# Head 0 of a graph attention layer aggregated in the last head's order

## The chip, the core and the metric

The kernel runs on one core of a Trainium2 chip. The time is the device time in microseconds of one execution; the number of a kernel is the median over several. TensorE is called PE in the profile (PEld its weight loads), VectorE DVE, ScalarE ACT, GpSimd POOL and SyncE SP. SP issues most DMAs.

## The reference, cut to what matters

There are 512 nodes of 768 features and 8704 edges. Two graph attention layers follow each other, the first with 8 heads of 768 features, the second with one; a residual and a layer norm close it.

```
h = (x @ W).reshape(n, H, C)
alpha_s = jnp.einsum('nhc,hc->nh', h, a_s)
alpha_d = jnp.einsum('nhc,hc->nh', h, a_d)
e = jax.nn.leaky_relu(alpha_s[src] + alpha_d[dst], NEG_SLOPE)
...                                     # softmax of e over the edges of each dst
msg = h[src] * alpha[:, :, None]
out = jax.ops.segment_sum(msg, dst, num_segments=n)
...
h = jax.nn.elu(gat_layer(x, W1, a_src1, a_dst1, b1, ...))
out = gat_layer(h, W2, a_src2, a_dst2, b2, ...)
x = layernorm(x + out)
```

## The kernel before

The edges are counted into a dense 512 x 512 matrix `cnt` (rows are dst, four tiles of 128), so a head's softmax is a dense one over rows and its aggregation a matrix product. Four steps belong to a head: the projection x W1, the logits (a product with a_s and a_d, summed along the features, on DVE), the softmax, and the aggregation, followed by elu and by the product with the head's 768 rows of W2, which is added into `h2`. All products are cut into 2 x 2 blocks (for heads 1 to 6 some into 3 x 3) and done with fewer block products than there are pairs of blocks. With 2 x 2 there are seven, P1 to P7; P1 and P2 take blocks of the operands as they are, and most of the others take sums and differences. Each block product sits in a PSUM bank of the pool `mm` (five banks); P2 is added into P1's bank, P4 into P7's and P3 into P5's.

The order of the work is written out by hand: each engine runs its instructions in the order in which the code issues them, and semaphores hold back an instruction whose inputs are not ready.

The softmax of one tile t goes through `lift` (the scores, ACT, L636), `leak` and `rank` (DVE, L640 and L645, with an exponential on ACT at L651), `weigh` (DVE, L879 to L883), a scaling on ACT (L899), a copy that splits the numbers in halves (L902), a transposing DMA on SP (L904) and `turn_in` (ACT, L907), which writes the tile's columns of `PT`. `rank` adds `absent`, which is large where there is no edge. It is made on ACT from `cnt`; for t = 2 at L566, from a difference that DVE takes at L565.

The aggregation of head 0 and of heads 1 to 6 is `mixed` (L949). It runs over c = 0, 1, 2, a chunk of 128 features in each half. `left_sums` (L932 to L935) makes sums of the head's features, `right_sums` (L943 to L946) sums of `PT`: t1, t2, the difference that is written over `PT`, and t4. P1 and P2 need only the columns `near` of `PT`, those of tiles 0 and 1; the sums need all four tiles. Per c the order on PE is P1, P6, P7, P2, P5, P4, P3. ACT copies P1 to `u` (L974); DVE adds P6 (L980) and P7 (into `w`, L981), subtracts `w` from P5 into the far half of `zr` (L986), adds `u` to P4 (L989) and subtracts `u` from P3 (L993). `elu` (L910) is two relus and an exponential on ACT (L916 to L918) and one DVE instruction into `gT` (L919). For the near half of the first chunk it is called at once; those of `zr` and of the far half of `u` are called in the next c:

```
            nc.scalar.copy(u, part("P1"))
            if h == c == 0:
                logarithm(slice(1, NT))
            if behind:
                behind = behind[0]()
            tt(u, u, part("P6"), op=ALU.add)
```

`logarithm` (L657) turns `cnt` into its logarithm, which the softmax of the later heads uses. ACT loads another table for it, and the old one again for the next exponential. In head 0 one tile of it stands in front of the stage and three behind the first copy to `u`.

Head 7 has a function of its own, `last_mixed` (L1001). It issues the sums of the right side first, then P1 of c = 0 and 1, then P2 of c = 0 and 1 with their elu, and then P6, P7, P5, P4 and P3 of c = 0 and 1, and c = 2 as a whole.

DVE work that isn't part of a head's aggregation is dealt into gaps: `half_logits` gives the two logits of one tile of the next head (L418). The logits of head 1's tile 2 are `some_logits`; those of tiles 0, 1 and 3 are `sources` (a_s) and `targets` (a_d). `row_out` (L622) sends the a_s logits through DRAM into a broadcast tile `q`: a small transpose on DVE (L625), four DMAs (L628) and one back (L631). On SP the loads of head 2's first weights (L109, L114) and vectors follow them.

After the aggregation of head 0 comes its product with W2 (`by_halves`, L409 in the profile), with sums on DVE (L389 to L392 for `gT`, L401 and L402 for the weights), and then the projection of head 2.

Of the kernel before, what the change touches and what calls it, by code (L numbers as in the profile page):

```python
# [13 lines left out]
AF = mybir.ActivationFunctionType  # L14
# [6 lines left out]
NO_EDGE = -1e30  # L21
# [16 lines left out]
def gat_pass(  # L38
# [16 lines left out]
    nc = tc.nc  # L55
    P = 128
    N, D = x.shape
    H = a_src1.shape[0]
    E = src.shape[0]
    NT = N // P  # L60
# [232 lines left out]
    far = const.tile([P, 1], F32, name="far")  # L293
# [75 lines left out]
    cnt = keep.tile([P, NT, N], F32, name="cnt")  # L369
    absent = keep.tile([P, NT, N], BF16, name="absent")  # L370
# [183 lines left out]
    def counted(t, ps):  # L554

        nc.scalar.copy(cnt[:, t, :], ps[:, :N])
        nc.scalar.activation(absent[:, t, :], ps[:, :N], AF.Relu, bias=far, scale=NO_EDGE)

    def counted_by_steps(t, ps):


        steps = ohp.tile([P, N + 1], F32, name="steps")
        nc.scalar.activation(steps[:, 1:], ps[:, :N], AF.Copy, scale=0.5)
        nc.scalar.activation(steps[:, :1], ps[:, N - 1:N], AF.Copy, scale=-0.5)
        nc.vector.tensor_tensor(cnt[:, t, :], steps[:, 1:], steps[:, :N], op=ALU.subtract)  # L565
        nc.scalar.activation(absent[:, t, :], cnt[:, t, :], AF.Relu, bias=far, scale=NO_EDGE)  # L566

    def first_projection(h, XA, B_, between):

# [63 lines left out]
    def lift(h, t):  # L633

        q = BC[h] if 0 < h < H and t + 1 == NT else qpool.tile([P, N], F32, name="q")
        nc.scalar.activation(q, BC[h][:, :N], AF.Identity, bias=AL[h][1][:, t:t + 1], scale=-1.0)  # L636
        return q
# [18 lines left out]
    def logarithm(tiles):  # L656
        nc.scalar.activation(cnt[:, tiles, :], cnt[:, tiles, :], AF.Ln, bias=tiny)  # L657
        folded.append(True)
# [19 lines left out]
    if not general:  # L678
# [12 lines left out]
        cps, done = {}, set()  # L691
# [82 lines left out]
        for n, batch in enumerate(batches):  # L774
            for k in sorted({c // quarter for c in batch} - made):
                destinations(k)
                made.add(k)
            if n + 1 < len(batches):
                sources(kinds(batch, False), waiting)
            if n + 2 == len(batches):  # L780
                sources(kinds(batches[-1], False), [])
            ahead = kinds(batches[n + 1], True) if n + 1 < len(batches) else []
            items_here = max(wants[n] - pos if n < len(wants) else 0, 1)
            share = len(ahead) // (items_here + 1) if n == 0 else -(-len(ahead) // items_here)
            waiting = []
            for f in extra.pop(n, []):
                f()
            while n < len(wants) and pos < wants[n]:
                if pos == wholes:
                    pairs = projection(1, XA, B1)  # L790
                    items += [(m, e, False) for m, e in pairs[:4]]
                multiply, empty, on_vector = items[pos]
                multiply()
                if on_vector:
                    waiting.append(empty)
                else:
                    empty()
                pos += 1
                for t, r in turns.get(pos, []):
                    turn_x(t, r)  # L800
                if pos == 1:
                    nc.scalar.activation(nidx, idx, AF.Copy, bias=0.5, scale=-1.0)
                part = 0 if n == 0 and pos == 2 else share
                for c in ahead[:part]:
                    one_hot(c, True)
                del ahead[:part]
            for c in ahead:
                one_hot(c, True)
            if n == 2:
                turn_b1()  # L810
            if n + 1 == len(batches):
                spread(0)
                q = [lift(0, t) for t in range(NT)]
                for t in range(NT - 1):
                    leak(q[t])
                for t in range(NT - 1):
                    rank(q[t], t)
            if n == 0:
                pst = mm.tile([P, 512], F32, name="mm")
                nc.tensor.matmul(pst[:1, :1], found, ones, start=True, stop=True)  # L820
            if n == 3:
                again = nc.values_load(flag[:1, :1], min_val=0, max_val=E)
            count(batch, n + 1 == len(batches))
        assert not extra and not waiting and pos == len(items) and len(done) == NT
    else:
# [26 lines left out]
        q = [lift(0, t) for t in range(NT)]  # L852
# [53 lines left out]
    def turn_in(t):  # L906
        nc.scalar.copy(PT.rearrange("p s n -> p (s n)").bitcast(U16).rearrange("p (s n h) -> p s n h", s=NT, h=2)[  # L907
            :, :, t * P:(t + 1) * P, :], parted.pop(t).rearrange("p (h s d) -> p s d h", h=2, s=NT))
# [40 lines left out]
    def mixed(h, A_, B_, fill, ends=()):  # L949

        tt = nc.vector.tensor_tensor
        behind = []

        def some(c, j):
            for f in fill[c][j]:
                f()

        for c in range(HK):
            u = work.tile([P, HN], F32, name="u")
            w = work.tile([P, HN], F32, name="w")  # L960
            zr = work.tile([P, N], F32, name="zr", bufs=3)
            bank = {}

            def part(p, over=None):
                if over is None:
                    bank[p] = mm.tile([P, 512], F32, name="mm")
                else:
                    bank[p] = bank[over]
                for k in range(2):
                    nc.tensor.matmul(bank[p][:, :HN], A_[p][:, k, c * P:(c + 1) * P], B_[p][:, k, :],  # L970
                                     start=over is None and k == 0, stop=k == 1, skip_group_check=True)
                return bank[p][:, :HN]

            nc.scalar.copy(u, part("P1"))  # L974
            if h == c == 0:
                logarithm(slice(1, NT))
            if behind:

                behind = behind[0]()
            tt(u, u, part("P6"), op=ALU.add)  # L980
            tt(w, u, part("P7"), op=ALU.add)  # L981
            for f in behind[:1]:
                f()
            near_l = elu(h, c, part("P2", over="P1"), near, "l")
            some(c, 0)
            tt(zr[:, far_], part("P5"), w, op=ALU.subtract)  # L986
            for f in behind[1:] + list(ends[:1]) * (c == HK - 1):
                f()
            tt(zr[:, near], u, part("P4", over="P7"), op=ALU.add)  # L989
            near_l()  # L990
            for f in list(ends[1:]) * (c == HK - 1):
                f()
            tt(u, part("P3", over="P5"), u, op=ALU.subtract)  # L993
            some(c, 1)

            def others(c=c, u=u, zr=zr):
                return [elu(h, HK + c, zr, slice(0, N), "r", spare=zr), elu(h, c, u, far_, "l", spare=u)]
            behind = [others]
        return behind[0]()

    def last_mixed(A_, B_, sums, fill):  # L1001

        h, tt = H - 1, nc.vector.tensor_tensor
        banks, us, nears = {}, {}, {}

        def part(c, p, over=None):
# [13 lines left out]
        def near_half(c):  # L1020
            nears[c] = elu(h, c, part(c, "P2", "P1"), near, "l")
# [8 lines left out]
            begin(c)  # L1030
        for c in range(2):
            near_half(c)
        behind = []
        for c in range(HK):
            if c == 2:
# [59 lines left out]
    AA, lsums = left_sums(0)  # L1095
    BB, rsums = right_sums()
    some_logits = half_logits(1, 2)

    def give(t):
        turn_out(q[t], t, weigh(q[t], t, scale=False))  # L1100

    done = {n: (lambda n=n: pairs[n][1]()) for n in range(4, 13)}
    beside = {4: [lambda: give(0)], 5: [done[4]], 6: [done[5]], 7: [done[6], lambda: give(1)],
              8: [done[7], lambda: leak(q[3]), lambda: rank(q[3], 3), lambda: turn_in(0)], 9: [lambda: give(2), done[8]],
              10: [lambda: give(3), lambda: turn_in(1), done[9]], 11: [done[10], lsums[0]],
              12: [done[11], lambda: turn_in(2), *lsums[1:3]], 13: [done[12], lambda: turn_in(3), lambda: logarithm(slice(0, 1)), *rsums[:2]]}
    for n in range(4, 14):
        pairs[n][0]()
        for f in beside[n]:
# [2 lines left out]
            load_w2(0, "w1")()  # L1112
            B2, pending = right(W2[0], "w1")
    pairs[13][1]()
    for f in rsums[2:]:
        f()
    besides = [lsums[3], *some_logits]

    def g_thirds(h):

# [53 lines left out]
    for h in range(H - 1):  # L1174
        last = h + 2 == H
        q = {}
        if 0 < h and not last:
            B3, rest_of_thirds, sums = load_thirds(h + 2)
# [8 lines left out]
        sources, targets = zip(*halves)  # L1187
        row = [lambda: row_out(h + 1)]
        if h == 0:
            GA, gsums = left(gT, gS)  # L1190
            finish = mixed(0, AA, BB, [[[besides[0], sources[1]], [besides[1], sources[0]]], [[], [sources[2]] + row + besides[2:]],
                                       [[], list(targets)]])
            load_w1(2)()
            load_a(2, a_src1[2], a_dst1[2])
            attend = attended(0)
# [8 lines left out]
            gsums[1]()  # L1204
            pending[0]()
            pairs[2][0]()
            gsums[2]()
            pairs[3][0]()
            gsums[3]()
            pending[1]()  # L1210
# [186 lines left out]

    first, second_, third_, fourth = (given(t) for t in range(NT))
    BB, rsums = right_sums()
    finish = last_mixed(AA, BB, [*rsums, lsums[3], lambda: nc.vector.memset(rows, 0.0)], {(1, 1): second_[:1], (2, 1): first})  # L1400
    every = slice(0, N)
    pairs = second(GA, B2)

# [28 lines left out]
    q, rden = {}, {}  # L1432
# [102 lines left out]
```

## Time and profile before

| what | us |
|---|---|
| median of 3 runs | 628.48 (627.97 to 628.87) |
| the profiled execution's own time | 628.25 |
| its span, first to last instruction | 626.5 |
| PE busy in the span | 615.7 |
| DVE busy | 528.8 |
| ACT busy | 339.2 |
| granted TensorE clock | 0.997 |

A row of the timeline reads: start, duration, engine, line, operation, output <- inputs, shapes, how many; a bracket gives the idle time of the engine in front and what ended it. A matmul of the code is two matmul instructions in the profile. A row of the waits reads: who waited for whom, microseconds in total, how often, the longest.

### The profile page before, as it was taken

To read this page: it belongs to the slowest core of one execution; us is meant where nothing else is said; L and a number is where in the kernel's file an instruction comes from. 1 tells how busy PE (TensorE), PEld (TensorE's weight loads), DVE (VectorE), ACT (ScalarE), POOL (GpSimd) and SP (SyncE) were. 2 spreads that over 40 slices of the span, in tenths; PEclk is the share of its full clock that TensorE was granted. 3 is DMA by queue.
4 is the path that set the end of the run, shared out by engine and by line. 5 is a ranking of instruction groups with operands and counts; after the bars stand their busy time and mean duration, and the time that the engine had idled before them with its cause. 6 is when DMAs were issued, how large, how long until landed. Compare 5 with 4: busy or idle time off the path is not lost.

```text
span 626.5 us, 8547 instructions
## 1 busy us (share of the span) xinstructions
PE 615.7 (98%) x2765; PEld 483.6 (77%) x2765; DVE 528.8 (84%) x1125; ACT 339.2 (54%) x602; POOL 148.9 (24%) x177
## 2 busy tenths in 40 slices
PE   8999999999999999999999999999999999999995
PEld 5555576556888888888888888888888888886553
DVE  8988979888899879978799778977898778978785
ACT  5874876650658236651658246751658146754361
POOL 1300011013333234323342323323342313010000
PEclk9999999999999999999999999999999999999998
DMA  8994297789999999999999998999999995590042
GB/s 298 326 235 110 67 265 238 188 216 267 249 222 142 326 256 198 172 274 219 248 237 175 308 250 194 194 283 226 228 215 192 317 280 91 107 261 17 17 76 79
DMA packets 109568, 129.45 MB, mean 207 GB/s; under 512 B 41622, under 2 KB 90446, under 8 KB 108750
## 3 DMA queue, kind: packets, MB, share of 16 engines
q1 hardware_dynamic: 75518, 91.35, 47.3%
q0 software_dynamic: 33568, 36.90, 38.4%
q10 hardware_dynamic: 432, 0.59, 0.3%
q8 instruction: 24, 0.39, 0.3%
q14 instruction: 26, 0.21, 0.1%
HBM read 99.84 MB, written 2.90 MB: 164 GB/s over the span
## 4 chain that ended last, share of the span: by engine, by line
PE 86%; ACT 1%; DMA 1%; DVE 1%; issue 0%
PE mm L480 46%; PE mm L970 20%; PE mm L409 13%; PE mm L1481 3%; PE mm L1012 3%; DMA zr<-pS 0%; DMA zr<-nr 0%; ACT PT L907 0%; ACT pS L902 0%; ACT q L899 0%; PE tr L1390 0%; ACT nr L902 0%; PE tr L891 0%; PE bc L1425 0%; DVE hs L1485 0%; PE tr L1427 0%
## 5 line engine op out<-in xcount | busy, mean ns | idle before, releaser
L486 ACT ACTIVATE hs<-mm 128x512 f32<-128x512 f32 x30 | 17.9, 596 | 86.1 <-PE mm L480 85.8
L970 PE MATMUL mm<-PT,hs 128*128 128x256 f32 x252 | 61.3, 379 | 0.0
L970 PEld LDWEIGHTS mm<-PT,hs 128*128 128x128 f32 x252 | 47.8, 190 | 7.3 <-ACT u L974 0.4
L649 ACT ACTIVATE q<-q,nmax 128x512 f32<-128x512 f32 x32 | 23.1, 721 | 51.2 <-DVE nmax L645 50.8
L493 DVE TENSOR_TENSOR hs<-hs,mm 128x512 f32<-128x512 f32 x45 | 30.9, 686 | 22.1 <-PE mm L480 21.3
L491 POOL DMA_DIRECT2D h<-pass x22 | 26.5, 1319 | 80.9 <-ACT pass L490 80.9
L970 PE MATMUL mm<-pS,gS 128*128 128x256 f32 x168 | 43.2, 380 | 1.3 <-DVE pS L944 1.3
L493 DVE TENSOR_TENSOR h<-h,mm 128x512 f32<-128x512 f32 x56 | 38.3, 684 | 6.3 <-PE mm L480 5.8
L907 ACT COPY PT<-zr 128x1024 uint16<-128x1024 uint16 x34 | 39.3, 1155 | 4.2 <-DMA zr<-pS 3.6
L480 PE MATMUL mm<-w2r,xT 128*128 128x256 f32 x160 | 37.8, 379 | 0.0
L480 PE MATMUL mm<-w2r,gT 128*128 128x256 f32 x160 | 37.0, 379 | 0.0
L970 PEld LDWEIGHTS mm<-pS,gS 128*128 128x128 f32 x168 | 31.8, 190 | 5.9 <-DVE pS L944 1.7
L133 POOL DMA_DIRECT2D w1t<-in_L_gnn_W_dram x18 | 29.2, 1642 | 30.4 <-PE mm L409 26.9
L480 PE MATMUL mm<-w1t,hs 128*128 128x256 f32 x144 | 34.1, 380 | 0.0
L480 PE MATMUL mm<-w1r,hs 128*128 128x256 f32 x144 | 34.1, 379 | 0.0
L480 PE MATMUL mm<-w1r,gS 128*128 128x256 f32 x144 | 34.0, 379 | 0.0
L480 PEld LDWEIGHTS mm<-w2r,gT 128*128 128x128 f32 x160 | 30.4, 190 | 4.1
L480 PEld LDWEIGHTS mm<-w2r,xT 128*128 128x128 f32 x160 | 30.4, 190 | 4.1
L974 ACT COPY u<-mm 128x256 f32<-128x256 f32 x21 | 7.8, 371 | 45.5 <-PE mm L970 45.5
L716 DVE TENSOR_SCALAR os<-nodes,idx 128x512 bf16<-128x512 f16 x104 | 29.3, 354 | 1.4 <-PE tr L742 1.4
L480 PEld LDWEIGHTS mm<-w1t,hs 128*128 128x128 f32 x144 | 27.3, 190 | 3.9 <-ACT absent L490 0.2
L480 PEld LDWEIGHTS mm<-w1r,hs 128*128 128x128 f32 x144 | 27.2, 190 | 3.8 <-DVE hs L1130 0.2
(294 smaller groups left out, 1560.8 us busy)
## 6 DMA issues: line engine op xcount, KB each, us to landing
w2r<-in_L_gnn_W_dram SPq DMA_DIRECT2D x48, 384.0 KB
w1r<-in_L_gnn_W_dram SPq DMA_DIRECT2D x43, 384.0 KB
gT<-xd SPq DMA_DIRECT2D x5, 1280.0 KB
w1t<-in_L_gnn_W_dram SPq DMA_DIRECT2D x24, 256.0 KB
h<-pass POOLq DMA_DIRECT2D x22, 256.0 KB, 4.6
w1t<-in_L_gnn_W_dram POOLq DMA_DIRECT2D x18, 256.0 KB, 6.2
w2t<-in_L_gnn_W_dram SPq DMA_DIRECT2D x15, 256.0 KB
w2t<-in_L_gnn_W_dram POOLq DMA_DIRECT2D x15, 256.0 KB, 9.1
```

Source lines behind the costliest of these rows:

```text
L133: nc.gpsimd.dma_start(o, i, accum_op=ALU.add)
L409: nc.tensor.matmul(ps[:, :HALF], A_[p][:, k, i * P:(i + 1) * P], B_[p][:, k, :], start=start and k == 0, stop=k == HK - 1, skip_group_chec ...
L480: nc.tensor.matmul(bank[chain][:, i * TH:(i + 1) * TH], A_[p][:, k, i * P:(i + 1) * P], B_[p][:, k, :], start=first and i == k == 0, stop= ...
L486: nc.scalar.activation(out(o), ps, AF.Copy, scale=sign)
L491: nc.gpsimd.dma_start(out(o), part, accum_op=ALU.add)
L493: nc.vector.tensor_tensor(out(o), out(o), ps, op=ALU.add if sign > 0 else ALU.subtract)
L649: nc.scalar.activation(q, q, AF.Exp, bias=nmax, scale=-1.0, accum_out=dens[t])
L716: nc.vector.tensor_scalar(o, nodes, idx[:, c:c + 1], None, op0=ALU.is_equal)
L907: nc.scalar.copy(PT.rearrange("p s n -> p (s n)").bitcast(U16).rearrange("p (s n h) -> p s n h", s=NT, h=2)[:, :, t * P:(t + 1) * P, :], p ...
L970: nc.tensor.matmul(bank[p][:, :HN], A_[p][:, k, c * P:(c + 1) * P], B_[p][:, k, :], start=over is None and k == 0, stop=k == 1, skip_group ...
L1012: nc.tensor.matmul(banks[c, p][:, :HN], A_[p][:, k, c * P:(c + 1) * P], B_[p][:, k, :], start=over is None and k == 0, stop=k == 1, skip_g ...
L1481: nc.tensor.matmul(ps[:, :cols.stop - cols.start], PT[:, s, t * P:(t + 1) * P], h2[:, s, cols], start=(s == 2), stop=(s == 1))
```

## The change

`last_mixed` becomes `near_first`, is called for head 0 as well as for head 7, and takes the head as an argument. For head 0 the right sums and the last left sum are issued first, and the logarithm of all four tiles stands on ACT behind the near halves of c = 0 and 1, in front of the far halves of c = 0. The logits of head 1 are dealt anew: both of tile 2 go behind the last `turn_in` in front of the evacuation of pair 13; a_s of tiles 3, 0 and 1 into c = 0, 1 and 2; `row_out` and a_d of tile 0 behind the last of them; a_d of tiles 1 and 3 into the product that follows. In the softmax of head 0, `absent` of tile 2 is issued behind the lifts of tiles 0 and 1 and no longer in front of them.

```diff
     def counted_by_steps(t, ps):
...
         nc.vector.tensor_tensor(cnt[:, t, :], steps[:, 1:], steps[:, :N], op=ALU.subtract)
-        nc.scalar.activation(absent[:, t, :], cnt[:, t, :], AF.Relu, bias=far, scale=NO_EDGE)
+        deferred.append(lambda: nc.scalar.activation(absent[:, t, :], cnt[:, t, :], AF.Relu, bias=far, scale=NO_EDGE))
...
                 spread(0)
-                q = [lift(0, t) for t in range(NT)]
+                q = [lift(0, t) for t in range(2)]
+                for f in deferred:
+                    f()
+                q += [lift(0, t) for t in range(2, NT)]
...
             nc.scalar.copy(u, part("P1"))
-            if h == c == 0:
-                logarithm(slice(1, NT))
             if behind:
...
-    def last_mixed(A_, B_, sums, fill):
-
-        h, tt = H - 1, nc.vector.tensor_tensor
+    def near_first(h, A_, B_, sums, fill):
+
+        tt = nc.vector.tensor_tensor
...
         for c in range(2):
             near_half(c)
+        if not h:
+            logarithm(slice(0, NT))
         behind = []
...
-              12: [done[11], lambda: turn_in(2), *lsums[1:3]], 13: [done[12], lambda: turn_in(3), lambda: logarithm(slice(0, 1)), *rsums[:2]]}
+              12: [done[11], lambda: turn_in(2), *lsums[1:3]], 13: [done[12], lambda: turn_in(3), *some_logits]}
...
     pairs[13][1]()
-    for f in rsums[2:]:
-        f()
-    besides = [lsums[3], *some_logits]
...
-            finish = mixed(0, AA, BB, [[[besides[0], sources[1]], [besides[1], sources[0]]], [[], [sources[2]] + row + besides[2:]],
-                                       [[], list(targets)]])
+            finish = near_first(0, AA, BB, [*rsums, lsums[3]], {(0, 1): sources[2:], (1, 1): sources[:1], (2, 1): [sources[1]] + row + [targets[0]]})
...
             pending[0]()
             pairs[2][0]()
+            targets[1]()
             gsums[2]()
+            targets[2]()
             pairs[3][0]()
...
-    finish = last_mixed(AA, BB, [*rsums, lsums[3], lambda: nc.vector.memset(rows, 0.0)], {(1, 1): second_[:1], (2, 1): first})
+    finish = near_first(H - 1, AA, BB, [*rsums, lsums[3], lambda: nc.vector.memset(rows, 0.0)], {(1, 1): second_[:1], (2, 1): first})
```

More of the change, by code (lines that the diff above doesn't have):

```diff
@@ L557, in counted @@
         nc.scalar.activation(absent[:, t, :], ps[:, :N], AF.Relu, bias=far, scale=NO_EDGE)
+    deferred = []
     def counted_by_steps(t, ps):
```

## The prediction

> **What bounds the kernel now.** I read the page's busy shares, then the waits of PE, then the chain of waits, then the timeline of two aggregations: head 0, which is changed, and head 7, which already has the order that head 0 gets.
>
> ```profile
> PE 615.7 (98%) x2765; PEld 483.6 (77%) x2765; DVE 528.8 (84%) x1125; ACT 339.2 (54%) x602; POOL 148.9 (24%) x177
> ```
> ```profile
> PE mm L970 <- DVE pS L944: 1.3, 1, 1.3
> ```
> ```profile
> 80.54 0.70 DVE pS L944
> 81.24 0.04 issue
> 81.28 1.13 PE mm L970 x4
> ...
> 86.14 13.22 PE mm L970 x60
> 99.35 54.30 PE mm L409 x168
> 153.65 18.20 PE mm L970 x84
> ...
> 549.18 18.18 PE mm L1012 x84
> ```
>
> PE is the bound: from 81.28 to 618.36 us the chain never leaves it, apart from 0.03 us of issue. Its only long wait in the middle is the 1.3 us for pS. An aggregation is 84 matmul instructions, four to each of 21 parts (7 products for each of three c), and takes 18.18 us at full pace: 0.866 us a part. Heads 1 to 6 reach that and so does head 7. Head 0 starts at 79.00 us and the next stage's first matmul is at 99.19: 20.19 us. So 20.19 - 18.18 = 2.0 us, 0.3% of the time, is all that the change can win, unless it speeds up something outside this stage. There PE has no gap left to close.
>
> Now the lines that carry the sum, from the timeline of head 7 and then of head 0.
>
> ```profile
> 549.02 3.62 PE L1012 MATMUL mm<-PT,hs 128*128 128x256 f32 x16
> 553.56 0.43 ACT L918 ACTIVATE nl<-nl 128x256 f32<-128x256 f32 x1
> 556.63 0.72 ACT L916 ACTIVATE nr<-zr,nb1T 128x512 f32<-128x512 f32 x1 [2.65 <-DVE zr L1052]
> 559.10 0.68 DVE L919 SCALAR_TENSOR_TENSOR gT<-nr,zr 128x512 f32<-128x512 f32 x1
> 559.71 0.42 DVE L1049 TENSOR_TENSOR zr<-mm,w 128x256 f32<-128x256 f32 x1
> 560.29 1.03 PE L1012 MATMUL mm<-PT,gS 128*128 128x256 f32 x4
> ```
> ```profile
> 79.80 1.28 ACT L657 ACT_TABLE_LOAD   x1
> 81.09 0.72 ACT L657 ACTIVATE cnt<-cnt,tiny 128x512 f32<-128x512 f32 x1
> 81.97 1.57 ACT L657 ACTIVATE cnt<-cnt,tiny 128x1536 f32<-128x1536 f32 x1
> 85.30 1.28 ACT L918 ACT_TABLE_LOAD   x1
> ```
>
> In head 7 ACT idles 2.65 us between the near halves and the far ones. Head 0 is to put the logarithm, with a table load on each side, into that gap.
>
> **The change, part by part.** Head 7's times are moved by 549.02 - 79.00 = 470.02 us.
>
> *Raw products in front.* P1 and P2 of c = 0 and 1 need only the first two softmax tiles, so PE has 4 x 0.866 = 3.46 us of work from 79.00 and wants P6 at 82.46. P6 needs the second right sum. On DVE the pair-12 evacuation starts at 77.54 as now; then come the two logits that are moved ahead of it (steps 1.00 and 0.88, rows of L418), the pair-13 evacuation (at 79.9) and the right sums from 80.4. The second starts 0.73 later (79.81 to 80.54 now) and ends at 81.8. P6 finds it 0.6 us early. The 1.26 us wait goes, and with it the waits at 82.41 and 86.14: -2.0 us.
>
> *First scores sooner.* ACT idles 1.44 us before absent (59.78); two lifts of 0.60 us go there. The ACT-bound softmax chain moves up by about 1 us, and the last turn_in, 78.62 to 79.79 now, ends near 78.7; SP's transposes and the loads behind them (77.19) move with it. Worth nothing: the right sums now wait for DVE until 80.4, so even 79.79 would do. Without that cover (0.6 us) a late turn_in would cost its excess.
>
> *A new wait on DVE.* After the right sums DVE still has L935 before it adds P6 and P7. By head 7's steps (0.61, 0.60, 0.60, then 0.9 to 1.06 for L935, 0.33, 0.33) w starts at 84.5 to 84.7 and ends near 85.05; P4 of c = 0 may start at 85.06. I take 0.1 us, between 0 and 0.3.
>
> *The logarithm.* This is the term that decides. ACT finishes the near half of c = 1 at 553.99 - 470.02 = 83.97. Then:
> - table load, 79.80 to 81.09 in its row: 1.29, to 85.26;
> - logarithm of 2048 columns: 0.72 for 512 and 1.57 for 1536 give 0.425 for each further 512, so 1.99, to 87.2;
> - two relus on zr, 0.76 and 0.72, to 88.7;
> - table load back, 1.29, to 90.0;
> - exponential, 0.61, to 90.6.
>
> Now gT of the first far half can start on DVE at 90.6. In head 7 that is 559.10, here 89.08. In the DVE queue the far subtraction of c = 1 (zr from P5) stands behind it: 90.6 + 0.61 = 91.2, and ends at 91.63. P3 of c = 1 writes into P5's bank and has to wait for that read: it starts at 91.7. Unhindered it would start at 560.29 - 470.02 = 90.27, or 90.37 with the 0.1. So PE waits 1.3 us. Before, the table came back at 86.59 and gT at 90.47 held nobody up.
>
> From 91.7, eight parts and 0.1 us to refill (86.14 to 87.11 took 0.97) end at 98.7. Against 99.19: **-0.5 us**. In terms: -2.0 + 0.1 + 1.3 + 0.1. If ACT overlaps its steps by 0.09 twice, -0.7; with the larger DVE steps, -0.3.
>
> The table load is where a page speaks against the change. The Trainium skill, "ScalarE: Activation LUTs", section "What ACT_TABLE_LOAD costs", puts a switch at about 1283 ns for the load and 1380 ns for a drain, 2.66 us in all. By that price the two switches would add 2 x 1.38 us to the chain above and the change would lose 2.3 us. The trace agrees with the load (1.28) and shows no such drain: the relu in front of 85.30 ended at 85.29, and the exponential behind it started at 86.59.
>
> *Behind the stage.* L401, which PE needs for P6 of the next product, is on time by 0.05 us now (105.54 + 1.35 against 106.94). Three logits stood ahead of the last gT; now two and the small transpose do, so gT starts 2.55 us after the stage's end, not 3.42, and L401 gains 0.87 us. The two other logits go behind L401; L402 then ends near 110.3 and is needed near 114.2. The score chain of head 1 starts 0.4 us later at most (fold_count 109.81 now); its right sums wait for the DVE queue until 138.75, while the last turn_in ends at 135.87. Nothing there reaches PE.
>
> *row_out moves* from c = 1 to c = 2. turned starts near 100.2, not 94.68, and everything behind it on SP (drow, q, the loads of head 2's first weights, the vectors) goes out 5.5 us later. The score row q is due for ACT near 107 and issued at 102.6. The DMA share falls from 1.11 to 0.29 at about 119.5, so these loads would be down by 125; PE wants them from 125.8, DVE at 126.6. I cost it at nothing; bounds are zero and the rival below.
>
> The profiled execution's own time was 628.25 us at a span of 626.5; the median of the three runs is 628.48. Minus 0.5: 627.75 for that execution, **628.0** as a median.
>
> **Rivals.**
> - *The far subtraction isn't held up* and head 0 runs at head 7's pace, plus 0.1: 99.19 - 97.28 = 1.9 us gained, 626.6. For it: head 7's own rows. Against: the queue order and five durations that the trace has. It needs the chain from 83.97 to 90.6 to be 1.3 us shorter. Chance 0.07.
> - *The switches cost more than their rows*: if ACT has to run dry around each, and pays the 1.28 us of the load twice over, the chain is 2.56 us longer, P3 of c = 1 starts at 94.3 and the stage ends at 101.3, 2.1 us later than now: 630.6. It loses from 0.25 us extra a switch (half of the forecast's 0.5). Against it: 85.29, 85.30, 86.59. Chance 0.07. The drain of the section cited above is this case.
> - *Head 1's transposes meet the late loads* (the slower side, by the SP queue). In before they run at 121.26 to 124.03 in a quiet stretch (DMA share 0.29). With loads until 125 they are slower: at 190.20 one that met a share of 1.1 to 1.3 was waited for until 198.70, 8.5 us. The last turn_in of head 1 may come 2.9 us late before DVE's right sum (138.75) notices, and 1.2 us more before P4's bank is not free, less PE's 0.5: it decides from 3.6 us. One slow transpose gives about that. If the first and the last are both slow, turn_in is 8.5 us late and PE loses 4.9: 633. Against: the last is issued near 131, when the loads are down. Chance 0.12.
>
> **How the numbers follow.** The forecast holds 0.74, with its own range 627.3 to 628.8 (the bounds above and the runs' spread, 627.97 to 628.87). About 0.2% (1.26 us) is what a measurement of this kernel can tell from no change, and -0.5 lies inside it. Within: 0.70 of the forecast's 0.74. Faster: 0.07 from the first rival and 0.01. Slower: 0.07 + 0.12 and 0.03 of the forecast's tail, 0.22. The range reaches to the first two rivals, 626.6 to 630.6, and leaves out 0.12.
>
> **What would show it.** Right: PE starts its second pair of parts without the 1.26 us wait; in the waits a PE line on DVE zr of about 1.3 us; a table load near 84.0 and one near 88.7; gT from nr behind an ACT wait near 90.6; the next product at 98.7. Wrong: that product at 97.3 (first rival), gaps beside the table loads (second), or a PE wait near 141 behind L448 (third). A wait on pS at 82.4 would mean that the logits ahead of the right sums cost more than I gave them.

## The result and the profile after

The changed kernel takes 629.80 us (median of 13 runs, 629.49 to 630.14), the kernel before 628.49 us (13 runs, 627.69 to 628.87). The ratio is 1.0023, with a 95% interval of 1.0015 to 1.0032: 1.3 us slower. The forecast was 628.0, 0.5 us faster. The profiled execution took 630.12 us at a span of 628.3 us.

The stage that the change rewrites did what the forecast said. The loss lies 30 us behind it. First the waits of PE; each row says who waited for whom, microseconds in total, how often, the longest:

```profile
PE mm L409 <- ACT hs L445: 1.7, 1, 1.7
PE mm L1015 <- DVE zr L1054: 1.3, 1, 1.3
```

The 1.3 us for pS is gone. The second row is the wait that the prediction put in its place. The first was not foreseen. (The aggregation of head 0 is now in `near_first`, L1015, that of heads 1 to 6 is L975; other line numbers behind the diff have moved by two to five: the far subtraction is L1054, `logarithm` L659, `elu` L921 to L924, the transposing DMA L909, `turn_in` L912.) The start of the stage and of the next one, from the timeline of before, and then the timeline of the stage after:

```profile
79.00 1.03 PE L970 MATMUL mm<-PT,hs 128*128 128x256 f32 x4
99.19 7.90 PE L409 MATMUL mm<-w1r,gT 128*128 128x384 f32 x24
```

```profile
79.24 3.62 PE L1015 MATMUL mm<-PT,hs 128*128 128x256 f32 x16
84.21 1.28 ACT L659 ACT_TABLE_LOAD   x1
85.51 2.00 ACT L659 ACTIVATE cnt<-cnt,tiny 128x2048 f32<-128x2048 f32 x1
88.88 1.28 ACT L923 ACT_TABLE_LOAD   x1
90.84 0.69 DVE L924 SCALAR_TENSOR_TENSOR gT<-nr,zr 128x512 f32<-128x512 f32 x1 [1.47 <-ACT nr L923]
91.92 1.13 PE L1015 MATMUL mm<-PT,gS 128*128 128x256 f32 x4 [1.29 <-DVE zr L1054]
98.93 1.45 PE L409 MATMUL mm<-w1r,gT 128*128 128x384 f32 x4
```

The stage takes 98.93 - 79.24 = 19.69 us, against 20.19 before: 0.50 less. It started 0.24 us later than before. The change is not needed to explain that: the shift is there from about 24 us on, and in two experiments below whose code is that of before up to this stage it starts at 79.19 and 79.50.

Now the chain of work that ended last, around the place of the first wait (start, microseconds, what):

```profile
91.92 7.19 PE mm L1015 x32
...
121.83 5.17 DMA zr<-pS
...
127.02 1.16 ACT PT L912
...
132.02 23.49 PE mm L409 x72
155.51 18.20 PE mm L975 x84
```

Before, this stretch was one row of PE, 99.35 to 153.65. Now the chain leaves PE for a transposing DMA of head 1's softmax and ACT's `turn_in`. Head 1's aggregation starts at 155.51 and not at 153.65; from there both kernels keep the same pace, and head 7's aggregation starts at 551.04 and 549.18, still 1.86 apart. The sum up to 155.51: +0.24 ahead of the stage, -0.50 in the stage, +0.14 from 98.93 to 126.28, where the projection of head 2 begins, and +1.98 from there (29.23 us against 27.25). That makes +1.86, the difference of the two profiled executions (630.12 - 628.25 = 1.87).

The rows of SP's queue and of ACT at that place, from the timeline of before and then of after:

```profile
94.92 1.29 SPq L628 DMA_DIRECT2D drow<-turned  x4
97.67 0.40 SPq L109 DMA_DIRECT2D w2t<-in_L_gnn_W_dram  x1
121.26 6.88 SPq L904 DMA_TRANSPOSE zr<-pS  x3
124.03 1.16 ACT L907 COPY PT<-zr 128x1024 uint16<-128x1024 uint16 x1
126.40 7.90 PE L409 MATMUL mm<-w2r,xT 128*128 128x384 f32 x24
128.53 0.48 ACT L445 COPY hs<-mm 128x384 f32<-128x384 f32 x1
```
```profile
100.70 1.29 SPq L630 DMA_DIRECT2D drow<-turned  x4
103.45 0.40 SPq L109 DMA_DIRECT2D w2t<-in_L_gnn_W_dram  x1
121.83 9.31 SPq L909 DMA_TRANSPOSE zr<-pS  x3
126.28 4.03 PE L409 MATMUL mm<-w2r,xT 128*128 128x384 f32 x12
127.02 1.16 ACT L912 COPY PT<-zr 128x1024 uint16<-128x1024 uint16 x1 [2.68 <-DMA zr<-pS]
131.50 0.85 ACT L445 COPY hs<-mm 128x384 f32<-128x384 f32 x2
132.02 4.14 PE L409 MATMUL mm<-w2r,xT 128*128 128x384 f32 x12 [1.71 <-ACT hs L445]
```

`row_out` (drow) and the loads of head 2's weights behind it on SP leave 5.8 us later. Head 1's first transpose is issued 0.57 us later than before but is waited for until 127.02 instead of 124.03: 5.2 us from issue to copy where it took 2.8. ACT's `turn_in` stands idle for it, 2.68 us. The copies of L445, which empty the PSUM banks of the projection of head 2, stand behind that `turn_in` in ACT's queue, with the scaling and splitting of two more tiles between them. The first ends at 131.98; PE, whose matmuls in front end at 130.31 (126.28 + 4.03), waits 1.71 us for its bank. Before, the copy ended at 129.01 and was wanted at about 130.28 (two products of 1.94 us behind 126.40): 1.27 us of slack, eaten by a delay of 3.0.

The windows show what the transpose meets. Behind the length of a window stand the busy microseconds of PE, PEld, DVE, ACT and POOL with their instructions in brackets, and the granted clock; the last two columns are the DMA share and GB/s. Before, then after:

```profile
120.00:124.00 4.00, 4.00 (x14) 2.41 (x13) 2.79 (x10) 3.70 (x6) 0.00 (x0) 1.00 0.29 66
124.00:128.00 4.00, 4.00 (x13) 2.29 (x13) 2.18 (x6) 3.91 (x5) 0.00 (x0) 1.00 0.29 66
```
```profile
120.00:124.00 4.00, 4.00 (x13) 2.20 (x12) 3.22 (x10) 3.93 (x7) 0.00 (x0) 1.00 1.12 266
124.00:128.00 4.00, 4.00 (x14) 2.39 (x13) 2.27 (x7) 1.32 (x2) 0.00 (x0) 1.00 1.00 194
```

Before, the transposes are alone (0.29). Now they share the engines with the late loads. ACT's busy time in the second window falls from 3.91 to 1.32 us of 4: it is waiting.

### The profile page after: what moved, and what is told of

Read it like the earlier page. It is cut to its first block, busy times and chain, and to the rows that moved or that the text cites. A ratio compares the mean times of both kernels' runs of the same rounds, so it can differ in the third digit from the quotient of the medians.

```text
span 628.3 us, 8544 instructions
## 1 busy us (share of the span) xinstructions
PE 615.9 (98%) x2765; PEld 483.8 (77%) x2765; DVE 528.0 (84%) x1125; ACT 339.2 (54%) x601; POOL 148.9 (24%) x177
## 4 chain that ended last, share of the span: by engine, by line
PE 90%; ACT 4%; DVE 3%; DMA 1%; issue 1%; DVEq 0%; ACTq 0%
PE mm L480 45%; PE mm L975 17%; PE mm L409 14%; PE mm L1015 4%; PE mm L1484 3%; PE held L409 2%; ACT os L716 1%; PE tr L744 1%; DMA zr<-pS 1%; PE mm L307 1%; PE held L610 1%; DVE scr L418 1%; PE bc L276 1%; PE bc L744 0%; ACT pS L907 0%
## 5 line engine op out<-in xcount | busy, mean ns | idle before, releaser
L975 PE MATMUL mm<-PT,hs 128*128 128x256 f32 x216 | 52.5, 379 | 0.0
L975 PEld LDWEIGHTS mm<-PT,hs 128*128 128x128 f32 x216 | 41.1, 190 | 5.8
L912 ACT COPY PT<-zr 128x1024 uint16<-128x1024 uint16 x34 | 39.3, 1155 | 6.0 <-DMA zr<-pS 5.4
L975 PE MATMUL mm<-pS,gS 128*128 128x256 f32 x144 | 37.0, 379 | 0.0
L133 POOL DMA_DIRECT2D w1t<-in_L_gnn_W_dram x18 | 27.8, 1566 | 31.1 <-DMA w1t<-in_L_gnn_W_dram 27.2
L975 PEld LDWEIGHTS mm<-pS,gS 128*128 128x128 f32 x144 | 27.4, 190 | 3.7
L480 PEld LDWEIGHTS mm<-w1r,gS 128*128 128x128 f32 x144 | 27.3, 190 | 3.7
```

What stands on the lines that cost most here:

```text
L133: nc.gpsimd.dma_start(o, i, accum_op=ALU.add)
L480: nc.tensor.matmul(bank[chain][:, i * TH:(i + 1) * TH], A_[p][:, k, i * P:(i + 1) * P], B_[p][:, k, :], start=first and i == k == 0, stop= ...
```

## The experiments

The theory (A, where an expectation uses letters): the late loads slow head 1's transposes, ACT's queue hands the delay on to PE, and since L445 then decides, the time that the logarithm's wait on zr costs would be swallowed there if that wait alone were cured. The rivals: the logarithm costs its time by itself, with or without the loads; the late loads hit PE in some other way than through ACT's queue. Each kernel was timed in five rounds against the kernel before; ratios are to that kernel, and the changed kernel itself has 1.0023. A difference of two ratios is turned into time with 628.5 us.

**The loads ahead of the aggregation.** Edit of the changed kernel:

```diff
+            load_w1(2)()
             finish = near_first(0, AA, BB, [*rsums, lsums[3]], ...)
-            load_w1(2)()
```

> The changed kernel with the loads of head 2's first weights issued on SP and POOL ahead of head 0's aggregation, so that they no longer stand behind row_out. Theory A (row_out's move sends these loads out 5.8 us later, they keep the DMAs busy at 122 to 127 us, head 1's first transpose takes 5.2 us instead of 2.8, ACT waits for it, and the copy L445 behind it frees a bank late): the DMA share is near zero at 122, the wait of PE on hs L445 (1.7 us) is gone, head 0's own gain of 0.5 us is left: 628.0 us, ratio to before 0.999. Theory B (the score chain of head 1 is late because of the logits put behind L401 and of the logarithm, whatever the loads do): the wait stays, 629.8 us, ratio 1.002.

Measured: 628.00 us, ratio 0.9997 (0.9988 to 1.0006). Timeline:

```profile
121.47 6.89 SPq L909 DMA_TRANSPOSE zr<-pS  x3
124.24 1.16 ACT L912 COPY PT<-zr 128x1024 uint16<-128x1024 uint16 x1 [0.26 <-DMA zr<-pS]
128.71 0.47 ACT L445 COPY hs<-mm 128x384 f32<-128x384 f32 x1
```

With the weights loaded before 116 us the transpose takes 2.8 us again, L445 is back at 128.71, and the wait of 1.7 us is gone; the wait on zr stays at 1.29. 0.0026 of the time, 1.6 us, come back. `drow` still leaves late here (100.33), so it is the loads of the first weights behind it that matter, not the row itself.

**The same loads, earlier, in the kernel before.**

```diff
+            load_w1(2)()
             finish = mixed(0, AA, BB, ...)
-            load_w1(2)()
```

> The kernel before with one edit: the loads of head 2's first weights issued ahead of head 0's aggregation. Theory A: before, nothing on PE waited for these loads or for the transposes, so there is nothing to win: 628.3 us, ratio 1.000. Rival (the DMAs of this stretch hold PE up in a way that the waits do not show): about 1 us faster, ratio 0.998.

Measured: 628.54 us, ratio 1.0002 (0.9993 to 1.0011). The edit is worth nothing where the loads were not late. What it brought above is the undoing of a loss, not a gain of its own.

**Only the later row, in the kernel before.**

```diff
-            finish = mixed(0, AA, BB, [[...], [[], [sources[2]] + row + besides[2:]],
-                                       [[], list(targets)]])
+            finish = mixed(0, AA, BB, [[...], [[], [sources[2]] + besides[2:]],
+                                       [[], [targets[0]] + row + list(targets[1:])]])
```

> The kernel before with one edit: row_out behind a_d of tile 0 in c = 2, about where the change puts it. Theory A: the loads of head 2 go out some 6 us later, the transposes of head 1 meet them, PE waits 1.5 to 2.5 us on L445: 630.3 us, ratio to before 1.003. Theory B: no such wait, 628.5 us, ratio 1.000.

Measured: 630.92 us, ratio 1.0041 (1.0027 to 1.0054). The waits of PE and the timeline:

```profile
PE mm L409 <- ACT hs L445: 1.8, 1, 1.8
```
```profile
121.77 10.13 SPq L904 DMA_TRANSPOSE zr<-pS  x3
127.78 1.16 ACT L907 COPY PT<-zr 128x1024 uint16<-128x1024 uint16 x1 [3.35 <-DMA zr<-pS]
```

The old order of the aggregation, the old place of the logarithm, the old logits in front, and still the new wait: moving `row_out` from c = 1 to c = 2 makes it by itself. `drow` leaves at 101.35 and the transpose takes 6.0 us. The cost is higher here, 0.41% or 2.6 us over 5 runs. This trace shows 2.1 us of it between the stage's end and head 1's aggregation (99.86 to 156.26 against 99.35 to 153.65); where the rest comes from was not looked into.

**The row in c = 1, in the changed kernel.**

```diff
-            finish = near_first(..., {(0, 1): sources[2:], (1, 1): sources[:1], (2, 1): [sources[1]] + row + [targets[0]]})
+            finish = near_first(..., {(0, 1): sources[2:], (1, 1): [*sources[:2]] + row, (2, 1): [targets[0]]})
```

> The changed kernel with a_s of tile 1 and row_out moved from c = 2 to c = 1. Theory A: the loads behind row_out go out about 5 us sooner, are down before head 1's transposes, and the wait of PE on hs L445 goes; the wait on zr (1.3 us) stays; two logits behind c = 1 cost PE at most 0.3 us: 628.0 to 628.3 us, ratio to before 0.999 to 1.000. Theory B (the deal of the logits, not the loads): 629.8 us.

Measured: 627.75 us, ratio 0.9990 (0.9981 to 0.9999). `drow` leaves at 95.38, the DMA share is back at 0.30 and 0.29 in the two windows, the wait for L445 is gone and that on zr stays (1.30). It is the reverse of the last experiment (a_s of tile 1, which the row needs, moves with it), and comes close to the 628.0 that was forecast for the whole change.

**The copies ahead of `turn_in`.** The loads stay late; ACT's order is changed. The first `turn_in` of head 1, the last transposing DMA and the loads that go with them are issued two products later, behind the L445 copies:

```diff
                 if n == 6:
-                    turn_in(0)
                     out_by_dma(2)
...
-                if n == 6:
-                    out_by_dma(3)
-                    B2, sums2, load_pairs, load_first, load_rest = load_second(1)
-                    load_pairs()
-                    load_first()
-                    load_rest()
...
                 pairs[n][1]()
+                if n == 1:
+                    turn_in(0)
+                    out_by_dma(3)
+                    B2, sums2, load_pairs, load_first, load_rest = load_second(1)
+                    load_pairs()
+                    load_first()
+                    load_rest()
```

> The changed kernel with the first turn_in and the last transpose of head 1 (and the loads behind it on SP) issued behind the two copies L445 of the next projection. The loads and the first transpose stay as late as they are. Theory A (PE waits because the copy stands behind the waiting turn_in in ACT's queue): the transpose still takes about 5 us, the wait on L445 goes, 628.0 to 628.3 us, ratio to before 0.999 to 1.000. Rival C (late transposes delay PE by way of the right sums too, so that the time is lost a few us later): a PE wait near 140 to 145, 629 us or more.

Measured: 627.92 us, ratio 0.9990 (0.9981 to 0.9999). Windows, then timeline:

```profile
120.00:124.00 4.00, 4.00 (x14) 2.23 (x13) 3.16 (x10) 3.94 (x7) 0.00 (x0) 1.00 1.12 260
124.00:128.00 4.00, 4.00 (x14) 2.41 (x13) 2.10 (x5) 1.95 (x3) 0.00 (x0) 1.00 1.22 226
```
```profile
128.35 0.48 ACT L445 COPY hs<-mm 128x384 f32<-128x384 f32 x1 [2.38 <-PE mm L409]
...
130.66 1.16 ACT L912 COPY PT<-zr 128x1024 uint16<-128x1024 uint16 x1
```

The DMA engines are as loaded as in the changed kernel, and the first `turn_in` runs even later (130.66). But L445 now waits for nothing but PE's product, and PE does not wait here at all. The row of `turn_in` can't show when the transpose landed, since it now stands behind the copies. The loads are as late as in the changed kernel and cost PE nothing here, so they hurt PE through the order of ACT's queue alone. The Trainium skill, "PSUM — Partial Sum Buffer", section "Engine vs sequencer instructions", calls ScalarE's queue strictly first in, first out. The traces agree: here the copy runs 2.13 us behind the start of its product (126.22 to 128.35); in the changed kernel its product was there by the same step at about 128.4 (126.28 + 2.13), and the copy ran at 131.50, behind the `turn_in` that had waited.

**The logarithm behind the stage.** It is issued in front of `fold_count(0)`, the first user of its result:

```diff
         for c in range(2):
             near_half(c)
-        if not h:
-            logarithm(slice(0, NT))
...
             pairs[3][1]()
+            logarithm(slice(0, NT))
             fold_count(0)
```

> The changed kernel with the logarithm moved on ACT from the aggregation to behind the copies L446 of the next product. Theory A: the wait of PE on zr (1.29 us) goes and the aggregation ends near 97.6 us, but the wait on L445 ends at a time that the transposes set, near 132, and grows from 1.7 to about 3.0 us; the total does not move: 629.8 us, ratio to before 1.002. Theory B (what is lost is lost by the logarithm's chain): about 1.3 us is won, 628.5 us, ratio 1.000.

Measured: 628.48 us, ratio 1.0002 (0.9993 to 1.0011). I had expected that the gain in the stage would be swallowed at L445, and 629.8 us. It was not; the time is the one that B gave. The chain of waits and the timeline:

```profile
79.34 18.13 PE mm L1015 x84
...
120.54 4.61 DMA zr<-pS
125.18 1.17 ACT PT L912
130.18 23.49 PE mm L409 x72
```
```profile
130.18 4.14 PE L409 MATMUL mm<-w2r,xT 128*128 128x384 f32 x12 [1.15 <-ACT hs L445]
```

The stage takes 18.13 us, full pace, with the logarithm (105.74 to 110.95 with its two table loads) outside it. And the wait for L445 did not grow by the 1.56 us won (19.69 - 18.13) but fell to 1.15. My reasoning took the loads and the transposes to stay where they were; but `row_out`, the loads (`drow` 99.08, not 100.70) and head 1's scores all hang on the end of the stage and move up with it. The two losses add.

**Both cures.** The logarithm behind the stage and the loads ahead of it, the edits above together.

> The changed kernel with both edits: loads ahead of the aggregation and logarithm behind L446. Theory A: no wait on zr and none on L445, the aggregation takes head 7's 18.2 us, 1.9 us less than before: 626.7 us, ratio to before 0.997. Theory B: one of the two waits stays or another takes its place, 628.0 to 628.5 us.

Measured: 626.80 us (626.36 to 627.42), ratio 0.9976 (0.9967 to 0.9985): faster than both kernels. The chain:

```profile
79.65 18.13 PE mm L1015 x84
...
152.54 18.21 PE mm L975 x84
```

PE waits neither for L445 nor for zr; a wait of 0.2 us for DVE (h, L448) is new with the logarithm's place. Against the changed kernel the loads alone take 0.0026 off the ratio (1.6 us), the logarithm alone 0.0021 (1.3 us), both together 0.0047 (3.0 us).

**The lifts back.** The one part of the change that is left, `absent` of tile 2 again ahead of all four lifts:

```diff
-                q = [lift(0, t) for t in range(2)]
                 for f in deferred:
                     f()
-                q += [lift(0, t) for t in range(2, NT)]
+                q = [lift(0, t) for t in range(NT)]
```

> The changed kernel with the first scores lifted as before: absent of tile 2 in front of all four lifts. Theory A (the right sums wait for DVE's logits until 80.6, so a last turn_in near 79.8 is as good as one at 79.0): no change against the changed kernel, 629.8 us, ratio to before 1.002. Rival (the earlier lifts are worth what they move, about 0.8 us): 630.6 us, ratio 1.0035, with a PE wait on pS near 82.5.

Measured: 630.04 us, ratio 1.0026 (1.0017 to 1.0035), not to be told from the changed kernel. The last `turn_in` in front of the stage starts at 78.42 instead of 77.83 (counted from the stage's start, 78.80 and 79.24, it comes 1.03 us later), and nobody waits for it: the right sums wait for DVE in both (80.15 and 80.59).

## Why the prediction was wrong

*Raw products in front* held. The right sums start at 80.59 (forecast 80.4), the second ends at 81.99, P6 starts at 82.69 without a wait. Where the logarithm is out of the way the stage takes 18.13 us, 2.06 less than before: the forecast's 2.0.

*First scores sooner* moved the last `turn_in` by 1.03 us (forecast: about 1) and is worth nothing, as costed.

*A new wait on DVE*, 0.1 us: P4 of c = 0 did not wait at all.

*The logarithm* held step by step: table loads at 84.21 and 88.88 (forecast 84.0 and 88.7, and the stage itself was 0.24 late), 2.00 us of logarithm (1.99), gT at 90.84 (90.6), the next product at 98.93 (98.7). The forecast counted PE's 1.3 us from the time at which P3 of c = 1 was due. That was 90.46 (89.60 + 0.86), it started at 91.92, so the like figure is 1.46; the profile books 1.29, since it counts from the end of the matmul in front. The refill behind it was 0.1 (91.92 to 92.88 is 0.96). So the terms were -2.06, 0, 1.46 and 0.10 against the forecast's -2.0, 0.1, 1.3 and 0.1. Both sums are -0.5: the mechanism is the forecast one, but that the sums agree so closely is luck, small errors that cancel. The first rival, no hold-up there, fell with it. So did the second: from the load at 84.21 to the next activation at 85.51 are 1.30 us, from 88.88 to 90.18 also 1.30. The drain of 1.38 us that the Trainium skill, "ScalarE: Activation LUTs", section "What ACT_TABLE_LOAD costs", adds to each switch is not there in this kernel.

*Behind the stage*: L401 starts at 104.36 against 105.54 before, 1.18 earlier or 0.92 earlier counted from the stage's end (forecast 0.87). The score chain of head 1 starts 0.58 us later (L664 at 110.39 against 109.81), where the forecast had 0.4 at most; the first transpose's 0.57 comes from there. The right sums of head 1 still wait for DVE (140.61) and not for the last `turn_in` (over at 137.73). PE needs 0.14 us more from the stage's end to the projection of head 2, which no run resolved.

***row_out moves*: "I cost it at nothing."** This is the step that failed. It cost 1.6 us by the run with the loads ahead and 2.1 us by the run with the row in c = 1 (0.0026 and 0.0033 of the ratio); without it these two stand at 628.00 and 627.75, about the forecast's 628.0. The mechanism was on the table as the third rival, with 0.12: loads 5.5 us later (5.8 measured), down by 125 (in the trace the share holds at 1.00 from 124 to 128), transposes slowed in that stretch. Two of its terms were wrong. The price came from one far row (8.5 us at 190 us); here the first transpose took 5.2. That row met more than the prediction said: its share of 1.1 to 1.3 is the mean of windows of ten microseconds, and in windows of two from 190 to 198 the share was 1.03, 1.38, 1.94 and 1.42. Above all the slack was counted at the wrong consumer. I followed `turn_in` to those who read `PT`, the right sums on DVE, and found 2.9 + 1.2 us. I did not ask what stands behind `turn_in` in ACT's own queue. There the L445 copies had 1.27 us, so the rival decides from 1.3 us late and not from 3.6, and a transpose of 5.2 us that would have been harmless by my sum was enough. The wait came at 130.31 behind L445, not near 141 behind L448. With the slack read there and the delay that was then measured, 5.2 - 2.8 + 0.57 = 3.0 us, less 1.27, the rival gives 1.7 us, and with the stage's -0.5 that is 1.2 us slower. The size of the delay could not be had from the trace of before: besides the row of 8.5 us it has a like one at 259.95, waited for until 267.32, 7.4 us.

The difference of the medians (1.31 us) is smaller than that of the two profiled executions (1.87). Of the changed kernel's 13 runs the profiled one (630.12) is the second slowest, that of before (628.25) lies under its median; 0.24 lay ahead of the stage. The slow transposes themselves took 5.17, 5.90, 5.98 and 4.61 us in the four traces whose chain runs through them (the changed kernel, the lifts back, the later row, the logarithm behind the stage), and PE's wait for L445 was 1.7, 2.4, 1.8 and 1.2. So a loss made of them need not be the same in every execution. That part was not measured further.

## What to carry to other kernels

In this kernel an ACT instruction that waited for a DMA held up the copy that stood behind it in ACT's queue, and through it PE. So: the slack of a late transfer is the least over what reads its result and over what is queued behind the reader, and the second is the one that is easily missed. When an edit moves the start of a train of loads, ask what quiet stretch it now ends in and who was using it. Two losses can be cured apart, and a stage that ends sooner carries its followers with it: what hangs on its end must not be held fixed in the sum.

## What the runs showed of the hardware

A transposing DMA of 128 x 1024 two-byte elements took 2.8 us from issue to the copy that waited for it while it was alone, and 4.6 to 6.0 us beside loads that kept the DMA share at 1.0 to 1.2; in the trace of before the one at 190.20, beside a share of 1.0 to 1.9, took 8.5 us, and the one at 259.95, beside 0.9 to 1.5, 7.4 us. The size of transfer and the instruction that issues it are the same. Moving the loads ahead, with nothing else changed, brought the 5.2 us back to 2.8.

A change of ACT's table cost its load and no more: 1.28 us for the load, 1.30 us from its start to the start of the next activation (84.21 to 85.51, 88.88 to 90.18).
